# A graph layer's scatters held to TensorE's products: four waits a slot put on the GpSimd queue

## The chip, the cores and the metric

The kernel runs on one core of one Trainium2 chip. The metric is the device time of one execution in microseconds (us), and the time of a kernel is the median of its runs. PE is TensorE (PEld its weight loads), DVE is VectorE, ACT is ScalarE, POOL is GpSimd, SP is SyncE, which here only issues DMAs.

## What is computed

A message-passing layer on a graph of 6250 nodes and 100000 edges, with 128 numbers a node and 128 an edge, and a normalised residual behind it:

```python
msg_in = concatenate([x[src], x[dst], edge_attr])   # 100000 x 384
h   = msg_in @ W + b
h   = (h - mean(h)) * rsqrt(var(h) + eps) * gamma + beta
msg = relu(h)
out = segment_sum(msg, src)                         # 6250 x 128
y   = layernorm(x + out)
```

The edges come sorted by `dst`, and are summed by `src`.

## The kernel before, in words

W is three blocks, one each for `x[src]`, `x[dst]` and the edge's own numbers. The kernel first multiplies all nodes by the first two blocks (`project`). Then it takes the edges in 782 tiles of 128. Four tiles are a **slot** (`PT = 4`), so there are 196 slots, `q` = 0 to 195. The tiles also fall into five **splits** of 164, 168, 168, 164 and 118 tiles.

In each slot `edges` makes, in one PSUM bank (`hp`, two banks in turn), the part of h that needs the edge and its `dst`: first four f32 products of the loaded edge tiles `eT` with W's third block (L523, which the profile shows as eight loads and eight products), then four bf16 products of a one-hot matrix with a window of the projected nodes (L527). `scatters` has ACT copy the bank into one of eight buffers in SBUF (`hs`, L535: buffer `q % 8`), and then POOL, for each of the four tiles, copies the tile's source numbers beside its rows (L539) and issues an indirect DMA (L540), which writes the 128 rows, of 528 bytes each, to their places in a table in DRAM (`sorted`), ordered by source block. The places come from a counting sort that DVE and PE work out ahead (`places`: steps of a generator, run at slots fixed in `steps_at`; L395 and L420 are its products).

When a split's rows are all in its table, the work on pairs of source blocks begins, five slots later (`LAG = 5`). There are 25 pairs a split. Such a pair loads its rows back (`hl`, L587 on SP), and on PE it has transposes (`turn`, L617), two groups of bf16 products that add the `src` part (`pick`, L632 and L636) and the f32 products that sum the messages by source (`sums`, L677). Between them DVE and ACT compare, square, scale and add. `work(n)` emits n steps of this pipeline. A step holds a fixed part of up to four pairs at different stages, and steps are dealt out to slots by `steps_due`, about 2.4 a slot.

All engines run in the order in which the program emits their instructions. One slot of the main loop emits: loads and windows on SP, the one-hot of slot q+2 on DVE, `edges(s, q)`, the first step of pair work, `scatters(s, q)`, the steps of `places` that are due, the other one or two steps of pair work. Splits 0 to 3 are worked on in this way under later slots; the last split's pairs follow in a tail (`tail`), with the final layer norm. POOL's part in the slots is the copies and scatters alone.

Waits are found by the framework from the data: a scatter waits for ACT's copy of its slot, for POOL's copy of the numbers and for its places; ACT's copy of slot q waits for the scatters of slot q - 8, which read the same buffer; and the load of a pair waits for all scatters of its split.

Of the kernel before, what the change touches and what calls it, by code (L numbers as in the profile page):

```python
# [17 lines left out]
D = 128  # L18
# [9 lines left out]
PT = 4  # L28
WN = 42
# [54 lines left out]
def fast_path(ctx, tc, io, bad_d):  # L84
# [3 lines left out]
    nc = tc.nc  # L88
# [3 lines left out]
    psum = ctx.enter_context(tc.tile_pool(name="psum", bufs=1, space=bass.MemoryType.PSUM))  # L92

    xb_d = [dram.tile([3, hi - lo, D], BF16, name=f"xb_d{k}") for k, (lo, hi) in enumerate(TABLES)]
    drel_d = dram.tile([PIECES, PT * P], BF16, name="drel_d")
    sorted_d = [dram.tile([NB * k * P + n * P, ROW], F32, name=f"sorted{s}")
                for s, (n, k, _, _) in enumerate(SPLITS)]
# [107 lines left out]
    w = const.tile([P, 3, D], F32, name="w")  # L205
# [22 lines left out]
    sloc = const.tile([P, TILES], F32, name="sloc")  # L228
# [78 lines left out]
    xa = tabs.tile([P, NB, 3 * D], BF16, name="xa")  # L307
# [157 lines left out]
    HS, DG = 8, 2  # L465
    hs_all = [const.tile([P, PT, ROW], F32, name=f"hs{i}") for i in range(HS)]
# [4 lines left out]
    def edge_loads(q, queue=None):  # L471

        if q % DG or q >= PIECES:
            return
        t0 = q * PT
        g = min(DG, PIECES - q)
        eT = edge.tile([P, DG * PT * P], F32, name="eT", bufs=3)
        db = edge.tile([P, DG * PT * P], BF16, name="db", bufs=3)
        for n in ([(0, g)] if q else [(i, 1) for i in range(g)]):
            c0, c1 = n[0] * PT * P, min((n[0] + n[1]) * PT * P, (TILES - t0) * P)  # L480
            nc.sync.dma_start(eT[:, c0:c1], io["eT"][:, t0 * P + c0:t0 * P + c1])
            c1 = (n[0] + n[1]) * PT * P
# [28 lines left out]
        nc.vector.tensor_scalar(oh[:, :m * P], db, part_w, None, op0=ALU.is_equal)  # L511
        held["oh", q] = oh

    def edges(s, q):
        t0 = q * PT
        m = min(PT, TILES - t0)
        c0 = q % DG * PT * P
        eT = held[q // DG][0][:, c0:c0 + m * P]
        oh, win = held.pop(("oh", q)), held.pop(("win", q))
        hp = psum.tile([P, PT, P], F32, name="hp", bufs=2)  # L520
        for j in range(m):
            at = slice(j * P, (j + 1) * P)
            nc.tensor.matmul(hp[:, j, :], eT[:, at], w[:, 2, :], start=j == 0, stop=False,  # L523
                             skip_group_check=True)
        for j in range(m):
            at = slice(j * P, (j + 1) * P)
            nc.tensor.matmul(hp[:, j, :], oh[:3 * WN, at], win[:3 * WN, :],  # L527
                             start=False, stop=j == m - 1, skip_group_check=True)
        held["hp", q] = hp

    def scatters(s, q):
        t0 = q * PT
        m = min(PT, TILES - t0)
        hs, hp = hs_all[q % HS], held.pop(("hp", q))
        nc.scalar.copy(hs[:, :m, 0:D], hp[:, :m, :])  # L535
        for j in range(m):
            t = t0 + j
            parts = P if t < TILES - 1 else LAST
            nc.gpsimd.tensor_copy(hs[:, j, D:D + 1], sloc[:, t:t + 1])  # L539
            i = nc.gpsimd.indirect_dma_start(  # L540
                out=sorted_d[s][:, :],
                out_offset=bass.IndirectOffsetOnAxis(ap=place_i[:parts, t:t + 1], axis=0),
                in_=hs[:parts, j, :], in_offset=None,
            )
# [38 lines left out]
    def load_pair(s, p):  # L583

        k = 2 * SPLITS[s][1]
        pair = late["blk"].tile([P, KMAX, ROW], F32, name="hl", bufs=4)
        nc.sync.dma_start(flat(pair[:, :k, :]),  # L587
                          dram_ap(sorted_d[s], p * k * P * ROW, [[k * ROW, P], [1, k * ROW]]))
        loaded[s, p] = pair

    class Pair:
# [17 lines left out]
        def turn(self):  # L609

            self.ohn = late["blk"].tile([P, KMAX, P], BF16, name="ohn", bufs=2)
            half = self.ohe.bitcast(BF16)
            for j0, m in [(0, self.k)]:
                tr = psum.tile([P, PT, P], F32, name="tr", bufs=BANKS["tr"]).bitcast(BF16)
                tr = tr.rearrange("p t (h d) -> p (t h) d", h=2)
                for j in range(m):
                    nc.tensor.transpose(tr[:, j, :], half[:, j0 + j, 1::2], ident_h)  # L617
                self.tr = tr

        def turned(self):  # L620
# [2 lines left out]
        def pick(self, g):  # L623

            j0, m = self.groups[g]

            name = "hp" if self.s == n_split - 1 and g % 2 else "sel"
            sel = psum.tile([P, PT, P], F32, name=name, bufs=BANKS[name])
            rows = self.hl[:, j0:j0 + m, 0:D]
            on_pe = g not in BY_DVE[self.s]  # L630
            if on_pe:
                nc.tensor.matmul(sel[:, :m, :], ident, rows, start=True, stop=False)  # L632
            for j in range(m):
                b = 2 * self.p + (j0 + j) % 2
                for i in range(3):
                    nc.tensor.matmul(sel[:, j, :], self.ohn[:, j0 + j, :],  # L636
                                     xa[:, b, i * D:(i + 1) * D],
                                     start=not on_pe and i == 0,
                                     stop=(j == m - 1 and i == 2) if on_pe else i == 2)
            self.sel[g] = sel  # L640

        def rest(self, g):
# [28 lines left out]
        def sums(self):  # L671
            k = self.k
            pa_t = psum.tile([P, 512], F32, name="pa")
            self.pa = pa_t[:, :2 * ACW].rearrange("p (h d) -> p h d", h=2)
            for h in range(2):
                for j in range(h, k, 2):
                    nc.tensor.matmul(self.pa[:, h, :], self.ohe[:, j, :], self.msg[:, j, :],  # L677
                                     start=(j == h), stop=(j == k - 2 + h))

        def add(self):  # L680
            b = 2 * self.p
# [70 lines left out]
    def run(g, n=1):  # L752
        for _ in range(n):
            next(g, None)
# [3 lines left out]
    for s in range(n_split):  # L758
        t = first_tile[s]
# [466 lines left out]
```

## Time and profile before

| | |
|---|---|
| median of 3 runs | 1448.1 us (1444.97 to 1451.01) |
| the profiled execution | 1445.61 us, of which the span from the first to the last instruction is 1443.8 us |
| mean granted clock of TensorE | 0.857 of full speed |
| PE, PEld | busy 1096.7 us (76%), 902.9 us (63%) |
| POOL | busy 1007.2 us (70%), of which 775.7 us are the 782 scatters |
| DVE, ACT | busy 950.8 us (66%), 610.9 us (42%) |
| first and last scatter | start at 25.8 us and at 1277.3 us |
| tail | from about 1275 us to the end, no scatters |

How to read it: the page is one profiled execution. A group's row gives line, engine, operation, the tiles written and read, the count, the busy time and the mean of one in ns, and behind the last bar the idle time of the engine just before these instructions, with what ended most of it. "issue" as a releaser means that the engine waited for nothing that the profile shows. In a table of windows each engine has its busy time and, in brackets, how many of its instructions ran in the stretch.

### The profile page before, as it was taken

Reading aid. Unit: us, or ns where it says so; the run is one execution under the profiler, and the core shown is the slowest. Engines: PE = TensorE matmul, PEld = TensorE weight load, DVE = VectorE, ACT = ScalarE, POOL = GpSimd, SP = SyncE. Lnnn points to the kernel's source line nnn. Section 1 sums busy time; section 2 is a strip of 40 time slices with the busy share of each in tenths; the row PEclk is TensorE's granted clock in tenths of the full one; section 3 lists DMA queues with packets and bytes.
Section 4 is the critical chain, followed back from the end, with each engine's and each line's share of the span. In section 5 each row is a group of like instructions: output and inputs, shape, how many; then the busy total and the mean of one; then the engine's idle time right before and its main releaser. Section 6 shows DMA issues by size and latency. Waiting matters only on the chain.

```text
span 1443.8 us, 28271 instructions
## 1 busy us (share of the span) xinstructions
PE 1096.7 (76%) x8918; PEld 902.9 (63%) x8918; DVE 950.8 (66%) x2511; ACT 610.9 (42%) x2658; POOL 1007.2 (70%) x1681
## 2 busy tenths in 40 slices
PE   4665544468788788787888888888878988999983
PEld 3654543346566676665766666767657777777762
DVE  7885553245556676675767676766777766778995
ACT  1332211023333344443443444434445555667983
POOL 3888878887877777777777777776777766622553
PEclk9877765567877989999998998888998999999997
DMA  6899653454555644555664556656554545433431
GB/s 200 239 272 287 196 164 120 137 179 143 165 171 168 192 158 154 186 178 184 187 205 158 166 165 191 196 164 196 180 172 153 185 158 173 137 99 117 139 123 55
DMA packets 122279, 245.85 MB, mean 170 GB/s; under 512 B 46555, under 2 KB 60396, under 8 KB 122118
## 3 DMA queue, kind: packets, MB, share of 16 engines
q1 hardware_dynamic: 95956, 189.83, 43.0%
q0 software_dynamic: 25184, 53.31, 10.6%
q8 instruction: 73, 1.20, 0.3%
q10 hardware_dynamic: 978, 0.80, 0.2%
q14 instruction: 88, 0.72, 0.2%
HBM read 155.74 MB, written 88.11 MB: 169 GB/s over the span
## 4 chain that ended last, share of the span: by engine, by line
PE 53%; issue 13%; DVE 11%; POOL 10%; DMA 6%; another core or an unknown queue 2%; ACT 2%; SPq 2%; POOLq 0%; ACTq 0%; DVEq 0%
PE pa L677 16%; PE sel L636 11%; PE hp L523 10%; PE sel L632 6%; POOL sorted L540 6%; PE tr L617 4%; DMA xs<-in_xblk 3%; PE hp L527 3%; DVE sc L383 3%; PE beside L420 2%; DVE msg L668 2%; DVE ohe L605 1%; POOL hs L539 1%; DMA db<-drel_d 1%
## 5 line engine op out<-in xcount | busy, mean ns | idle before, releaser
L540 POOL DMA_INDIRECT sorted<-hs,place_i x782 | 775.7, 992 | 315.3 <-issue 221.8
L677 PE MATMUL pa<-msg,ohe 128*128 128x130 f32 x1900 | 316.0, 313 | 47.4 <-issue 29.0
L535 ACT COPY hs<-hp 128x512 f32<-128x512 f32 x196 | 113.9, 581 | 561.1 <-DMA sorted<-hs,place_i 156.9
L523 PE MATMUL hp<-w,eT 128*128 128x128 f32 x1564 | 276.9, 323 | 96.7 <-ACT hs L535 62.1
L677 PEld LDWEIGHTS pa<-msg,ohe 128*128 128x128 f32 x1900 | 272.5, 217 | 75.2 <-issue 56.4
L523 PEld LDWEIGHTS hp<-w,eT 128*128 128x128 f32 x1564 | 238.6, 228 | 115.7 <-ACT hs L535 67.5
L636 PEld LDWEIGHTS <-ohn 128*128 128x128 bf16 x2850 | 186.3, 101 | 162.8 <-issue 143.2
L653 ACT ACTIVATE sq<-sel 128x128 f32<-128x128 f32 x875 | 230.3, 282 | 108.9 <-PE sel L636 54.0
L636 PE MATMUL sel<-xa,ohn 128*128 128x128 bf16 x2625 | 214.3, 226 | 59.1 <-issue 46.9
L668 DVE SCALAR_TENSOR_TENSOR msg<-sel,rstd,cut 128x128 f32<-128x128 f32 x875 | 247.0, 344 | 8.7
L605 DVE TENSOR_TENSOR ohe<-hl,beside 128x1024 f32<-128x1024 f32 (+1 forms) x125 | 144.7, 1159 | 144.4 <-PE sel L636 47.8
L653 ACT ACTIVATION_READ_ACCUMULATOR sq<-sel 128x1 f32 x875 | 186.8, 213 | 0.0
L646 DVE TENSOR_TENSOR sel<-sel,hl 128x512 f32<-128x512 f32 x100 | 69.4, 694 | 153.2 <-remote 80.4
L539 POOL COPY hs<-sloc 128x1 f32<-128x1 f32 x782 | 165.2, 211 | 3.8
L621 ACT COPY ohn<-tr 128x1024 bf16<-128x1024 bf16 (+1 forms) x125 | 120.7, 965 | 89.9 <-PE hp L527 44.8
L632 PE MATMUL sel<-hl,ident 128*128 128x512 f32 (+1 forms) x250 | 137.1, 631 | 4.7 <-issue 3.9
L617 PE MATMUL tr<-ident_h,ohe 128*128 128x128 bf16 x950 | 93.6, 233 | 42.2 <-issue 29.6
L511 DVE TENSOR_SCALAR ohd<-db,part_w 128x512 bf16<-128x512 bf16 x194 | 70.9, 366 | 58.3 <-PE hp L527 31.3
L527 PE MATMUL hp<-win,ohd 126*128 126x128 bf16 x782 | 91.6, 240 | 13.0 <-issue 7.0
L617 PEld LDWEIGHTS <-ohe 128*128 128x128 bf16 x950 | 65.0, 104 | 56.6 <-issue 42.0
L527 PEld LDWEIGHTS <-ohd 126*128 126x128 bf16 x782 | 70.4, 110 | 25.2 <-issue 17.2
L656 ACT ACTIVATE std<-ss,eps 128x4 f32<-128x4 f32 (+1 forms) x250 | 74.3, 297 | 8.1
(157 smaller groups left out, 937.1 us busy)
## 6 DMA issues: line engine op xcount, KB each, us to landing
hl<-sorted SPq DMA_DIRECT2D x100, 528.0 KB
eT<-in_eT SPq DMA_DIRECT2D x96, 512.0 KB
sorted<-empty SPq DMA_DIRECT2D x125, 198.0 KB
db<-drel_d SPq DMA_DIRECT2D x96, 256.0 KB
sorted<-hs,place_i POOLq DMA_INDIRECT x782
hl<-sorted SPq DMA_DIRECT2D x25, 396.0 KB
win<-xb_d SPq DMA_DIRECT2D x196, 31.5 KB
xb_d<-xb SPq DMA_DIRECT2D x16, 384.0 KB
```

Of the source, the lines that this page charges most:

```text
L523: nc.tensor.matmul(hp[:, j, :], eT[:, at], w[:, 2, :], start=j == 0, stop=False, skip_group_check=True)
L527: nc.tensor.matmul(hp[:, j, :], oh[:3 * WN, at], win[:3 * WN, :], start=False, stop=j == m - 1, skip_group_check=True)
L539: nc.gpsimd.tensor_copy(hs[:, j, D:D + 1], sloc[:, t:t + 1])
L540: i = nc.gpsimd.indirect_dma_start(out=sorted_d[s][:, :], out_offset=bass.IndirectOffsetOnAxis(ap=place_i[:parts, t:t + 1], axis=0), in_=h ...
L605: nc.vector.tensor_tensor(self.ohe[:, :k, :], self.hl[:, :k, D:D + 1].to_broadcast([P, k, P]), row_bc(iota_p, k), op=ALU.is_equal)
L617: nc.tensor.transpose(tr[:, j, :], half[:, j0 + j, 1::2], ident_h)
L621: nc.scalar.copy(self.ohn[:, :self.k, :], self.tr[:, :self.k, :])
L632: nc.tensor.matmul(sel[:, :m, :], ident, rows, start=True, stop=False)
L636: nc.tensor.matmul(sel[:, j, :], self.ohn[:, j0 + j, :], xa[:, b, i * D:(i + 1) * D], start=not on_pe and i == 0, stop=(j == m - 1 and i = ...
L653: nc.scalar.activation(sq[:, j, :], self.sel[g][:, j, :], AF.Square, accum_out=ss[:, j:j + 1])
L668: nc.vector.scalar_tensor_tensor(self.msg[:, j0 + j, 0:D], self.sel[g][:, j, :], rstd[:, j:j + 1], cut, op0=ALU.mult, op1=ALU.max)
L677: nc.tensor.matmul(self.pa[:, h, :], self.ohe[:, j, :], self.msg[:, j, :], start=(j == h), stop=(j == k - 2 + h))
```

## The change

`scatters` is parted. `evict` keeps ACT's copy, and puts the slot's four tiles into a list, `waiting`. `scatter(n, tied)` takes n tiles from the head of the list and emits for each POOL's copy of its source numbers and its indirect DMA, as before. With `tied` the DMA gets one more dependency: on the last PE product that was emitted up to there (`pe` notes each product of the slots).

In slots 21 to 185 the four tiles of slot q - 1 are scattered in slot q, one at each of four points, each tied:

1. after the four f32 products of slot q (L523),
2. after its four bf16 products (L527),
3. after the first step of pair work, ahead of ACT's copy of slot q,
4. after the slot's steps of `places` and its other steps of pair work.

Slots 0 to 19 and 187 to 195 scatter their own tiles at once, untied. Slot 20 scatters nothing, and slot 186 scatters the four tiles of slot 185 and its own. The orders of PE, DVE, ACT and SP are what they were. On POOL, too, the copies and scatters come in the same order.

```diff
-    def edges(s, q):
+    def edges(s, q, half):
...
-            nc.tensor.matmul(hp[:, j, :], eT[:, at], w[:, 2, :], start=j == 0, stop=False,
-                             skip_group_check=True)
+            pe(nc.tensor.matmul(hp[:, j, :], eT[:, at], w[:, 2, :], start=j == 0, stop=False,
+                                skip_group_check=True))
+        half()
...
-    def scatters(s, q):
+    def evict(s, q):
         t0 = q * PT
         m = min(PT, TILES - t0)
         hs, hp = hs_all[q % HS], held.pop(("hp", q))
         nc.scalar.copy(hs[:, :m, 0:D], hp[:, :m, :])
-        for j in range(m):
-            t = t0 + j
+        waiting.extend((s, q, j) for j in range(m))
+
+    TIE = (20, 186)
+    waiting = []
+
+    def scatter(n, tied):
+
+        for s, q, j in waiting[:n]:
+            t = q * PT + j
             parts = P if t < TILES - 1 else LAST
-            nc.gpsimd.tensor_copy(hs[:, j, D:D + 1], sloc[:, t:t + 1])
+            nc.gpsimd.tensor_copy(hs_all[q % HS][:, j, D:D + 1], sloc[:, t:t + 1])
             i = nc.gpsimd.indirect_dma_start(
...
+            if tied:
+                tc.add_manual_dep(i.ins, last_pe[0].name, written, reason="rows behind products")
...
+        del waiting[:n]
...
             edge_hot(q + 2)
-            edges(s, q)
+            tied = TIE[0] < q < TIE[1]
+            edges(s, q, (lambda: scatter(1, True)) if tied else lambda: None)
+            if tied:
+                scatter(1, True)
             n = steps_due(q + 1) - n_steps
             work(min(n, 1))
-            scatters(s, q)
+            if tied:
+                scatter(1, True)
+            evict(s, q)
+            if not TIE[0] <= q < TIE[1]:
+                scatter(len(waiting), False)
             for g in steps_at.pop(q, []):
                 run(g)
             work(n - 1)
+            if tied:
+                scatter(len(waiting) - PT, True)
```

More of the change, by code (lines that the diff above doesn't have):

```diff
@@ L94, in fast_path, with pe @@
     xb_d = [dram.tile([3, hi - lo, D], BF16, name=f"xb_d{k}") for k, (lo, hi) in enumerate(TABLES)]
+    written = mybir.DependencyInfo(mybir.DependencyClass.Sync, mybir.DependencyReason.DATA)
+    last_pe = [None]
+    def pe(i):
+        last_pe[0] = i.ins
+        return i
     drel_d = dram.tile([PIECES, PT * P], BF16, name="drel_d")
@@ L522, in edges @@
             at = slice(j * P, (j + 1) * P)
-            nc.tensor.matmul(hp[:, j, :], eT[:, at], w[:, 2, :], start=j == 0, stop=False,
-                             skip_group_check=True)
+            pe(nc.tensor.matmul(hp[:, j, :], eT[:, at], w[:, 2, :], start=j == 0, stop=False,
+                                skip_group_check=True))
+        half()
         for j in range(m):
             at = slice(j * P, (j + 1) * P)
-            nc.tensor.matmul(hp[:, j, :], oh[:3 * WN, at], win[:3 * WN, :],
-                             start=False, stop=j == m - 1, skip_group_check=True)
+            pe(nc.tensor.matmul(hp[:, j, :], oh[:3 * WN, at], win[:3 * WN, :],
+                                start=False, stop=j == m - 1, skip_group_check=True))
         held["hp", q] = hp
-    def scatters(s, q):
+    def evict(s, q):
         t0 = q * PT
@@ L542, in scatters @@
                 out_offset=bass.IndirectOffsetOnAxis(ap=place_i[:parts, t:t + 1], axis=0),
-                in_=hs[:parts, j, :], in_offset=None,
+                in_=hs_all[q % HS][:parts, j, :], in_offset=None,
             )
+            if tied:
+                tc.add_manual_dep(i.ins, last_pe[0].name, written, reason="rows behind products")
             tc.declare_no_dep(i.ins, group=f"scatter{s}", reason="rows of different edges")
@@ L616, in turn @@
                 for j in range(m):
-                    nc.tensor.transpose(tr[:, j, :], half[:, j0 + j, 1::2], ident_h)
+                    pe(nc.tensor.transpose(tr[:, j, :], half[:, j0 + j, 1::2], ident_h))
                 self.tr = tr
@@ L635, in pick @@
                 for i in range(3):
[L636 to L639, printed above, removed]
+                    pe(nc.tensor.matmul(sel[:, j, :], self.ohn[:, j0 + j, :],
+                                        xa[:, b, i * D:(i + 1) * D],
+                                        start=not on_pe and i == 0,
+                                        stop=(j == m - 1 and i == 2) if on_pe else i == 2))
             self.sel[g] = sel
@@ L676, in sums @@
                 for j in range(h, k, 2):
-                    nc.tensor.matmul(self.pa[:, h, :], self.ohe[:, j, :], self.msg[:, j, :],
-                                     start=(j == h), stop=(j == k - 2 + h))
+                    pe(nc.tensor.matmul(self.pa[:, h, :], self.ohe[:, j, :], self.msg[:, j, :],
+                                        start=(j == h), stop=(j == k - 2 + h)))
         def add(self):
```

## The prediction

> **What bounds the kernel now.** I read the page first, for the chain and the groups.
>
> ```profile
> span 1443.8 us, 28271 instructions
> ...
> POOL 3888878887877777777777777776777766622553
> ...
> PE 53%; issue 13%; DVE 11%; POOL 10%; DMA 6%; another core or an unknown queue 2%; ACT 2%; SPq 2%; POOLq 0%; ACTq 0%; DVEq 0%
> ...
> L540 POOL DMA_INDIRECT sorted<-hs,place_i x782 | 775.7, 992 | 315.3 <-issue 221.8
> ```
>
> PE carries half of the chain, and 13% of it is "issue": PE idle with no wait to show for it. POOL is 10%, but it is busy for most of every slice until 1275 us. So I cut the span into stages by windows, and asked who waits in each.
>
> ```profile
> 100.00:410.00 310.00, 180.65 (x1145) 149.50 (x1143) 143.91 (x302) 71.33 (x222) 248.62 (x413) 0.71 0.56 174
> 410.00:1200.00 790.00, 658.25 (x5534) 537.71 (x5533) 534.63 (x1366) 350.21 (x1594) 579.14 (x969) 0.90 0.56 177
> 1200.00:1275.00 75.00, 65.57 (x596) 53.34 (x596) 47.34 (x135) 42.41 (x201) 49.89 (x86) 0.92 0.43 140
> ```
>
> ```profile
> ACT hs L535 <- DMA sorted<-hs,place_i: 144.9, 29, 8.4
> ...
> PE hp L523 <- ACT hs L535: 62.1, 20, 5.9
> ```
>
> These two waits are of 100 to 410 us. **Stage one** belongs to POOL: the scatters go back to back, ACT waits for buffers that they still read, and PE waits for ACT. The timeline, read slot by slot, has POOL seven slots behind ACT from slot 13 on (slot 30's products ran at 157.7 to 159.1 us, slot 29's scatters began at 206.2), and it has caught up at slot 64, at 408 us.
>
> **Stage two**, 410 to 1200 us, is the changed one. A scatter follows ACT's copy by a few us, and POOL pauses about every second slot. Who is late then? PE's own rows say:
>
> ```profile
> PE sel L636 <- issue: 33.5, 98, 0.5
> PE pa L677 <- issue: 25.2, 76, 1.0
> ...
> PE beside L395 <- DVE cnt L392: 11.5, 4, 4.2
> ```
>
> All "issue" rows of PE in this stage add to 98 us, all waits for other engines to 26 us. The timeline shows what such an issue wait looks like. First a group of 12 products that runs freely, then one that doesn't, then POOL beside the second:
>
> ```profile
> 691.36 0.83 PE L636 MATMUL sel<-xa,ohn 128*128 128x128 bf16 x12
> ```
>
> ```profile
> 711.97 0.33 PE L636 MATMUL sel<-xa,ohn 128*128 128x128 bf16 x3 [0.22 <-issue]
> 712.70 0.44 PE L636 MATMUL sel<-xa,ohn 128*128 128x128 bf16 x5 [0.39 <-issue]
> 713.45 0.39 PE L636 MATMUL sel<-xa,ohn 128*128 128x128 bf16 x4 [0.32 <-issue]
> 714.19 0.39 PE L636 MATMUL sel<-xa,ohn 128*128 128x128 bf16 x4 [0.35 <-issue]
> ```
>
> ```profile
> 711.00 0.98 POOL L540 DMA_INDIRECT sorted<-hs,place_i  x1 [0.28 <-POOL hs L539]
> 711.99 0.19 POOL L539 COPY hs<-sloc 128x1 f32<-128x1 f32 x1
> 712.46 0.98 POOL L540 DMA_INDIRECT sorted<-hs,place_i  x1 [0.28 <-POOL hs L539]
> ```
>
> The 12 products took 0.83 us; then about four came every 0.73 us, which is half of POOL's cycle of 0.98 + 0.19 + 0.28 = 1.45 us. To see whether it is POOL, I counted PE's weight loads in windows where the scatters do not pause:
>
> ```profile
> 615.00:639.00 24.00, 20.55 (x184) 16.40 (x183) 14.73 (x42) 8.70 (x40) 19.76 (x32) 1.00 0.49 154
> 646.00:664.00 18.00, 10.55 (x86) 7.99 (x84) 12.59 (x27) 6.20 (x30) 14.61 (x26) 0.95 0.60 201
> 926.00:948.00 22.00, 18.57 (x148) 14.52 (x145) 13.43 (x36) 8.02 (x40) 18.05 (x29) 0.92 0.49 153
> 1062.00:1085.00 23.00, 14.43 (x112) 9.80 (x109) 13.72 (x32) 5.63 (x28) 18.49 (x33) 0.93 0.43 138
> ```
>
> 521 loads in 87 us: 6.0 a us. The whole of stage two has 5533 in 790 us, 7.0 a us. POOL's idle time before its scatters there is 208.8 us for 485 of them (its group in that window); less the 0.28 us between copy and scatter each time (136 us), 73 us are true pauses, 64 of them longer than 0.1 us. So stage two is 717 us of scattering at 6.0 loads a us, 4300, and 73 us of pause, which give the other 1230: 17 a us. PE lives on POOL's pauses: a pause lets it run ahead, and the scatters starve it again. I read this as cause, not coincidence, since the stalls keep step with the scatters; the trace alone doesn't prove it.
>
> **The change, part by part.**
>
> *Order of work.* PE, DVE, ACT and SP emit what they did; evict stays where the scatters stood. Cost nothing. Each tied scatter moves past one slot of PE work. Behind it on POOL wait only later copies and scatters (POOL has no other work until the tail). Two wait for its landing. ACT's copy of slot q needs the scatters of slot q - 8, now let go in slot q - 7: six slots remain, 39 us at 6.5 us a slot, against a scatter some 8 us late. The loads of a split's rows on SP come five slots after it (first rows of split 1: issued at 564.9 us, their last scatter began at 535.7). One slot of these five goes. If that cover failed, SP's queue would stop with all edge loads behind it: in stage one SP waited 24 us so, once, and that stays.
>
> *The wait itself.* One more semaphore a scatter. The scatter's row has 806 semaphore instructions for 782 scatters, 17 ns in the median. In stage two a wait that is met costs that at most, in the shadow of the 0.28 us from copy to scatter; the 0.28 us stands in the rows with one such instruction as with a longer first one. In stage one POOL is the bound, so there it would count: slots 21 to 63, 172 scatters, 172 x 0.017 = 3 us if not hidden, 172 x 0.28 = 48 us if each tied wait cost a gap of its own. I take 0, since the gap is one of latency; 48 stays for the range. PE's signals at four more points: nothing, as L636's products that signal keep the group's pace; no row excludes a few us either way.
>
> *Stage one's ties.* Nothing else: PE is six slots past each of them, so they are met before POOL arrives.
>
> *Stage two's ties.* Slots 65 to 185 hold 484 scatters, or 484 x 1.45 = 702 us of POOL, and the change removes none. PE's loads stay 5533. By the two rates, stage two = scattering + pause, and only what PE gets out of a us of pause can alter it. The ties make three differences.
>
> First, where POOL pauses. Before, it stops for ACT's copy; now, mostly for the fourth point, the end of a slot, since the first three come within 3 us of its start and POOL needs 1.45 us for each. PE, freed by the pause, then runs to that point. That is the same trade.
>
> Second, POOL no longer works ahead while PE waits for another engine. Before, it did: tiles that were copied were scattered, and PE lost nothing. Now a PE held by DVE holds POOL too, and such a pause feeds nobody. The waits are 26 us; those of the sort's products (L395, L420: 17 us) lie ahead of the fourth point, and about half of the other 9. POOL is there waiting as often as it has caught up, 64 slots of 121. So (17 + 4.5) x 0.53 = 11 us are lost. Bounds: 0, if POOL is always behind, and 26.
>
> Third, a gain is possible: pauses may become shorter and more frequent, each at an empty queue of PE. At 17 loads a us against the free group's 12 in 0.83 us (14 a us, with what it saves up coming on top) I see no large reserve, and take 0. Its bound is in the rivals.
>
> *A rule.* The page "SBUF — State Buffer" of the Trainium skill says, under "Who interferes with whom", that PE and ACT never wait on anyone. By it the scatters couldn't slow PE, the 98 us of issue waits would be PE's own, and the sum here would be 0, with 1446 us. The rows of 711 us speak against it.
>
> *End.* From slot 186 nothing is tied. POOL then holds one slot more than before only if it was ahead; before, slot 184's last scatter ended at 1203.2 us, PE reaches slot 186 at 1203.4. The tail starts as it did: 0.
>
> Sum, against the profiled execution: 1445.6 + 11 = 1457 us. The median of the three runs lies 2.5 us over that execution, so I forecast **1458 us**.
>
> **The rivals.**
>
> *Slower by the lost pauses* (my forecast), 1458, with 1448 to 1477 as its bounds (0 to 26 us in stage two, 0 to 3 us in stage one, on 1448).
>
> *No change.* POOL's work and PE's loads are the same, and the freed PE reaches each point as soon as before it reached ACT's copy. For it: in the sum only the rate per us of pause counts. Against: the 26 us of waits. 1448.
>
> *Faster.* One mechanism: PE's issue waits. A tie gives PE a quarter slot of progress before every scatter, so it is not starved in runs of ten and more scatters. At most the 98 us could come back, but POOL needs 4 x 1.45 = 5.8 us of a slot's 6.5, so a slot can shrink by 0.7 us at most, 85 us in 121 slots. A quarter of the 98 us would be 1424. It decides once pauses come in nearly every slot and one us of them gives clearly more than 17 loads. Against it: the rate needs empty queues at the right moments, and nothing places the ties so.
>
> *Much slower.* The tied wait is not hidden and stage one grows by up to 48 us: 1496. For it: that stage has no reserve. Against: the gap of 0.28 us is the same in all rows.
>
> That the ties do nothing is true of stage one, 43 of the 165 tied slots, and is in the sum.
>
> **How the numbers follow.** About 0.5%, 7 us, is what a measurement of this kernel can tell from no change. Slower by the lost pauses 0.42, no change 0.24, faster 0.27, much slower 0.07. Part of the first case stays under 7 us, and part of the no-change case exceeds it, which about cancels: slower 0.49, within 0.24, faster 0.27. The range runs from 1422, the faster case's price, to 1482, a little over the upper bound of the first, towards the last; my own case alone would be 1448 to 1477.
>
> **What would show it.** Right: stage one's end stays near 408 us at slot 64; in 410 to 1200 us POOL's idle time before its scatters grows by about 11 us and names PE; loads per us of unbroken scatters stay near 6; ACT's copy waits for no scatter. Wrong: PE's issue waits fall well below 98 us in that stage at a shorter span (the faster case), the copy-to-scatter gap grows beyond 0.28 us in stage one, or SP's wait for a split's rows shows up behind slot 83, 125 or 166.

## The result, and the profile after

The changed kernel takes **1426.84 us** (four runs, 1423.71 to 1427.48) against 1447.28 us of the kernel before on the same chip (1444.97 to 1451.01). The ratio is **0.9852, with a 95% interval of 0.9826 to 0.9878**: faster by 20 us, where 1458 us, slower by 10, was forecast. The page of after, the lines that answer to those of before:

```profile
span 1425.2 us, 28435 instructions
...
POOL 3888878888777777777777777777777667623543
...
PE 55%; issue 14%; DVE 11%; DMA 8%; POOL 6%; SPq 4%; ACT 2%; another core or an unknown queue 1%; POOLq 0%; ACTq 0%; DVEq 0%
...
L555 POOL DMA_INDIRECT sorted<-hs,place_i x782 | 778.5, 996 | 296.4 <-issue 139.3
```

The span is 18.6 us shorter. The scatters cost what they did (778.5 us for 782), and POOL's idle time before them fell from 315.3 to 296.4 us, 18.9 us. On the chain POOL went from 10% to 6%, while "issue" did not shrink: 14% after 13%. So POOL gave something up and PE's issue waits stayed. The stages say where. Windows of after, one for each stage (columns: span, then busy time and count of PE, PEld, DVE, ACT, POOL, then the granted clock, the DMA share and GB/s):

```profile
100.00:410.00 310.00, 181.05 (x1128) 149.71 (x1126) 143.20 (x299) 71.34 (x229) 247.83 (x411) 0.69 0.57 173
410.00:1180.00 770.00, 639.81 (x5522) 523.85 (x5519) 534.27 (x1368) 349.97 (x1584) 574.74 (x965) 0.92 0.59 181
1180.00:1257.00 77.00, 67.96 (x634) 56.93 (x633) 49.41 (x142) 42.86 (x202) 54.71 (x94) 0.93 0.45 144
```

Stage one is as it was (POOL busy 247.83 us, before 248.62; PE 181.05 and 180.65). Slot by slot: slot 65 starts at 408.9 us in both kernels; slot 186 starts at 1184.1 us, before at 1203.4. All of the gain, 19.3 us, lies in the 121 slots between, and none in the tail (241.1 us from slot 186 to the end, before 240.4). These 121 slots, before and after:

```profile
408.90:1203.40 794.50, 662.00 (x5569) 540.14 (x5568) 538.22 (x1376) 353.87 (x1612) 582.79 (x975) 0.90 0.56 176
```

```profile
408.90:1184.10 775.20, 644.53 (x5572) 527.69 (x5569) 538.77 (x1377) 353.71 (x1603) 578.10 (x971) 0.92 0.58 181
```

The same 5568 loads are done in 19.3 us less. Who waits in stage two? First PE's waits of after in 410 to 1180 us, then POOL's there (line, releaser: us in total, times, longest):

```profile
PE sel L653 <- issue: 36.3, 93, 1.1
PE pa L694 <- issue: 22.0, 60, 1.1
PE tr L634 <- issue: 19.6, 50, 1.1
...
PE beside L402 <- DVE cnt L399: 8.1, 6, 2.8
```

```profile
POOL sorted L555 <- issue: 87.6, 277, 4.1
POOL sorted L555 <- POOL hs L554: 26.0, 90, 0.6
POOL sorted L555 <- PE sel L653: 22.4, 33, 1.5
POOL sorted L555 <- PE hp L535: 16.8, 24, 1.6
POOL sorted L555 <- PE tr L634: 9.7, 14, 1.3
```

All issue rows of PE add to 100 us (98 before), its waits for other engines to 23 (26 before). By its wait rows PE stalls as much as it did; what fell is its busy time in the 121 slots, 662.00 to 644.53 us for the same products. A stall shows in busy time too: the 16 products from 711.97 us on in the prediction's timeline are busy for 1.55 us, 0.10 each, the 12 of the free group for 0.07 each. What changed on POOL is who ends its pauses: now PE's products, and sooner. I read the length of each pause off the records: the time between two scatters beyond the 0.475 us of copy and gap, where it exceeds 0.1 us. In the 121 slots:

| | before | after |
|---|---|---|
| pauses | 64 | 77 |
| together, us | 81 | 63 |
| mean of one, us | 1.27 | 0.82 |
| 121 slots, us | 794.5 | 775.2 |
| 121 slots less pauses, us | 713.5 | 712.2 |

POOL's scatters with their copies are a fixed 712 us, and the 18 us of pause that are gone are the gain. That is bookkeeping: where POOL's work is fixed, any gain has to show as less pause. What made it, the experiments have to say.

### The profile page after: what moved, and what is told of

Read it like the earlier page. It is cut to its first block, busy times and chain, and to the rows that moved or that the text cites. A ratio compares the mean times of both kernels' runs of the same rounds, so it can differ in the third digit from the quotient of the medians.

```text
span 1425.2 us, 28435 instructions
## 1 busy us (share of the span) xinstructions
PE 1078.0 (76%) x8918; PEld 889.3 (62%) x8918; DVE 951.5 (67%) x2511; ACT 612.0 (43%) x2658; POOL 1006.2 (71%) x1681
## 4 chain that ended last, share of the span: by engine, by line
PE 55%; issue 14%; DVE 11%; DMA 8%; POOL 6%; SPq 4%; ACT 2%; another core or an unknown queue 1%; POOLq 0%; ACTq 0%; DVEq 0%
PE pa L694 16%; PE hp L530 11%; PE sel L653 10%; PE sel L649 6%; PE tr L634 4%; DMA xs<-in_xblk 4%; PE hp L535 3%; POOL sorted L555 3%; DVE sc L390 2%; DVE ohe L622 2%; DMA sorted<-hs,place_i 2%; PE beside L427 2%; DVE msg L685 2%; POOL y L719 1%; POOL y L759 1%
## 5 line engine op out<-in xcount | busy, mean ns | idle before, releaser
L555 POOL DMA_INDIRECT sorted<-hs,place_i x782 | 778.5, 996 | 296.4 <-issue 139.3
L530 PE MATMUL hp<-w,eT 128*128 128x128 f32 x1564 | 268.8, 315 | 101.4 <-ACT hs L543 60.7
L694 PE MATMUL pa<-msg,ohe 128*128 128x130 f32 x1900 | 307.8, 311 | 42.1 <-issue 24.6
L530 PEld LDWEIGHTS hp<-w,eT 128*128 128x128 f32 x1564 | 230.0, 220 | 121.6 <-ACT hs L543 65.1
L653 PEld LDWEIGHTS <-ohn 128*128 128x128 bf16 x2850 | 182.9, 99 | 163.6 <-issue 148.1
L653 PE MATMUL sel<-xa,ohn 128*128 128x128 bf16 x2625 | 209.0, 223 | 63.1 <-issue 55.7
L638 ACT COPY ohn<-tr 128x1024 bf16<-128x1024 bf16 (+1 forms) x125 | 120.7, 966 | 115.6 <-PE hp L535 53.4
L554 POOL COPY hs<-sloc 128x1 f32<-128x1 f32 x782 | 161.2, 206 | 3.8
L634 PE MATMUL tr<-ident_h,ohe 128*128 128x128 bf16 x950 | 90.3, 231 | 43.1 <-issue 27.3
L535 PEld LDWEIGHTS <-ohd 126*128 126x128 bf16 x782 | 69.1, 108 | 24.4 <-issue 18.9
```

Source lines behind the costliest of these rows:

```text
L530: pe(nc.tensor.matmul(hp[:, j, :], eT[:, at], w[:, 2, :], start=j == 0, stop=False, skip_group_check=True))
L535: pe(nc.tensor.matmul(hp[:, j, :], oh[:3 * WN, at], win[:3 * WN, :], start=False, stop=j == m - 1, skip_group_check=True))
L554: nc.gpsimd.tensor_copy(hs_all[q % HS][:, j, D:D + 1], sloc[:, t:t + 1])
L555: i = nc.gpsimd.indirect_dma_start(out=sorted_d[s][:, :], out_offset=bass.IndirectOffsetOnAxis(ap=place_i[:parts, t:t + 1], axis=0), in_=h ...
L634: pe(nc.tensor.transpose(tr[:, j, :], half[:, j0 + j, 1::2], ident_h))
L638: nc.scalar.copy(self.ohn[:, :self.k, :], self.tr[:, :self.k, :])
```

## The experiments

**What they are to tell apart.** Theory A: the waits end POOL's pauses sooner, after a quarter slot of PE's work and not after ACT's copy, and a shorter pause serves PE as well. Theory B: the waits do nothing; the gain comes from emitting the scatters a slot later, at four places. Theory C: the gain belongs to one of the four points alone. Behind them stands a question that the prediction left open: do the scatters cause PE's issue waits?

The chips differ: the kernel before took 1477.2 us on the one of the first four experiments (the second chip, below) and 1346.5 to 1347.5 us on those of all others, so every ratio is against the kernel before on the same chip. A profile of the kernel before was taken on the first chip alone.

### Which wait does it

`x1_untied` emits everything at the four points but adds no wait:

```diff
-            if tied:
+            if False:
                 tc.add_manual_dep(i.ins, last_pe[0].name, written, reason="rows behind products")
```

> The changed kernel with the scatters emitted at the four points, but without the added waits. Theory A (the gain is in POOL's pauses, which now end at a product of PE and no longer at ACT's copy): no wait, no gain, the time of the kernel before, 1447 us within 5, and POOL's idle time before its scatters back near 209 us in stage two. Rival B (emitting the scatters a slot later is the change, not the wait): 1427 us. Rival C (TensorE's granted clock happened to be better): the clock decides, near 0.87 and 1427 us.

`x2_first` ties only the scatter at point 1 (`scatter(1, False)` at points 2 and 3, `False` at the fourth):

> Only the first of the four points is tied (the four f32 products of the next slot); the other three scatters follow freely. One hold a slot in place of four. Theory A, if any hold that ends at a PE product will do: near 1427 us, with pauses once a slot. If the pause must also be cut into parts: half the gain, about 1437. Rival C: no order in the times, clock and time move together.

`x3_last` ties only what is let go at point 4:

> Only the fourth point is tied, the end of a slot's pair work. By the working of the prediction POOL stands there most often, so this one wait should carry nearly all of the effect: 1427 to 1432 us. If several short holds are what counts: about 1437 us.

`x4_three` ties points 1 to 3, not the fourth:

```diff
-                scatter(len(waiting) - PT, True)
+                scatter(len(waiting) - PT, False)
```

> Points one to three are tied, the fourth is free. If the fourth point carries the effect: 1440 us and more. If holds at any point do: 1427 to 1432 us.

Measured, ratios to 1477.2 us:

| | us | ratio, 95% interval | slots 65 to 164, us | pauses there: number, us | PE's issue waits there, us |
|---|---|---|---|---|---|
| x1_untied | 1476.57 | 0.9987 [0.9956, 1.0017] | 665.4 | 53, 84.7 | 115 |
| x2_first | 1454.23 | 0.9846 [0.9791, 0.9900] | 653.1 | 59, 66.7 | 101 |
| x3_last | 1455.39 | 0.9871 [0.9811, 0.9931] | 646.4 | 61, 61.9 | 98 |
| x4_three | 1447.96 | 0.9809 [0.9753, 0.9864] | 644.9 | 60, 59.9 | 100 |
| before, first chip | 1447.28 | 1 | 646.9 | 49, 61.9 | 84 |
| after, first chip | 1426.84 | 0.9852 [0.9826, 0.9878] | 633.4 | 60, 45.5 | 89 |

Theory B falls with x1: the later emission alone gives nothing that shows. Theory C falls with x2 and x3: either end of the slot, alone, gives as much as the whole change did on the first chip, and three points give about as much. It takes a wait on PE once a slot; which product it is matters little. Whether more holds give a little more is not settled: x4 lies 6 us under x2, its four runs at 1446.17 to 1451.76 us and those of x2 at 1451.74 to 1455.76. POOL's group of scatters in slots 65 to 164 (its idle time stands behind the second bar), x1 and then x3:

```profile
L555 POOL DMA_INDIRECT sorted<-hs,place_i x397 | 393.3, 991 | 193.6 <-issue 148.2 <-POOL hs L554 39.9 <-ACT hs L543 2.2
```

```profile
L555 POOL DMA_INDIRECT sorted<-hs,place_i x399 | 394.1, 988 | 166.4 <-issue 103.7 <-POOL hs L554 32.4 <-ACT hs L543 13.9
```

27.2 us less idle time before as many scatters; the slots are 19.0 us shorter (the pauses by my count 22.8). In every row of the table the slots' time less the pauses is 581 to 588 us: that is 400 scatters at 1.455 us, 582 us, which the change can't touch. These slots take that sum and what POOL pauses.

On PE's side this chip shows what the first didn't: its issue waits fall with the ties. In slots 65 to 185 they are 132 us in x1 and 116, 111 and 114 in x2 to x4, that is 16 to 21 of the 20 to 29 us by which these slots are shorter (818.6 us in x1, then 798.6, 790.1 and 790.1).

The granted clock went up beside the gain on the first chip (0.90 to 0.92 in the slots). It doesn't make the gain, as runs at a like mean clock over the span show: on the first chip one run of the changed kernel had 0.855 and took 1426.71 us, where the kernel before took 1445.61 at 0.857; on the second chip runs at 0.843 took 1483.33 us before, 1453.42 in x2 and 1448.21 in x4.

**Why a shorter pause is enough.** For each pause in slots 65 to 185 I counted the loads that it gave: all loads from its start to the start of the next pause, less 6.0 for each us between them in which POOL scattered. By chip, since the two stall unequally (first chip: before and after; second: x1 to x4; 137 of 141 and 298 of 306 pauses, as the last ones of each profile are left out):

| pause, us | first chip: pauses, mean us | loads it gave | a us | second chip: pauses, mean us | loads it gave | a us |
|---|---|---|---|---|---|---|
| 0.1 to 0.5 | 28, 0.21 | -1.3 | | 44, 0.22 | 1.8 | |
| 0.5 to 0.8 | 34, 0.71 | 18.6 | 26 | 16, 0.69 | 12.8 | 19 |
| 0.8 to 1.1 | 21, 0.96 | 22.4 | 23 | 76, 0.98 | 19.5 | 20 |
| 1.1 to 1.4 | 12, 1.27 | 27.9 | 22 | 85, 1.22 | 18.5 | 15 |
| 1.4 to 1.7 | 29, 1.58 | 24.7 | 16 | 36, 1.58 | 21.6 | 14 |
| 1.7 to 2.2 | 11, 1.82 | 26.3 | 14 | 24, 1.89 | 19.0 | 10 |
| over 2.2 | 2, 3.59 | 38.5 | 11 | 17, 2.84 | 26.7 | 9 |

Single pauses scatter widely (standard deviations of 9 to 15 loads). The trend is the same on both chips all the same: up to about 1 us the yield grows, and from there to 2 us it hardly does, 22 to 28 loads on the first chip and 19 to 22 on the second. On the first chip the short pauses are mostly those of after and the long ones those of before, so length isn't parted there from the place at which a pause falls. Before, a pause ended with ACT's copy (47 of the 64 ended 0.7 to 0.8 us after the copy's end), which stands behind a group of products and ACT's squares of it; of its 64 pauses 34 were of 1.5 us and more, and what lay beyond 1 us bought little. After, four are so long. One pause of each kind, in the timelines of POOL, before and then after (start, duration, instruction, in brackets the idle time ahead):

```profile
737.71 0.98 POOL L540 DMA_INDIRECT sorted<-hs,place_i  x1 [2.05 <-issue]
```

```profile
1139.72 0.98 POOL L555 DMA_INDIRECT sorted<-hs,place_i  x1 [1.23 <-remote]
1140.71 0.19 POOL L554 COPY hs<-sloc 128x1 f32<-128x1 f32 x1
1141.17 0.98 POOL L555 DMA_INDIRECT sorted<-hs,place_i  x1 [0.28 <-PE hp L530]
...
1146.23 0.98 POOL L555 DMA_INDIRECT sorted<-hs,place_i  x1 [0.97 <-remote]
```

The 2.05 us of the first are 1.77 us beyond the usual gap of 0.28; those after are 0.95 and 0.69 beyond it, 6.5 us apart. The same can be read by time. From the start of a pause to 7 us behind its end PE issued 8.1 loads a us, before and after; later than that, 5.2. More pauses and shorter ones leave less of the late time: 289 us of the 121 slots before, 236 after. The table of yields fits a stock of instructions that fills in a pause and is used up under the scatters; no record shows such a stock, so that is an inference.

### Do the scatters cause the stalls?

`x5_none` takes the kernel before and issues no scatters in slots 65 to 165:

```diff
+            if 64 < q < 166:
+                continue
             i = nc.gpsimd.indirect_dma_start(
...
-                          dram_ap(sorted_d[s], p * k * P * ROW, [[k * ROW, P], [1, k * ROW]]))
+                          dram_ap(sorted_d[0 if s < 4 else s], p * k * P * ROW, [[k * ROW, P], [1, k * ROW]]))
```

> The kernel before without the scatters of slots 65 to 165 (POOL only copies the source numbers there; pairs of splits 1 to 3 read back split 0's rows, so that all that is read has been written). If the scatters starve PE: PE's issue waits of 98 us in stage two fall below 20 us in the slots without scatters, and those 101 slots take about 5.6 us each in place of 6.6, so the span falls by 80 to 120 us. If PE's issue waits are its own: they stay, and the span falls by less than 20 us.

`x6_memset` puts two memsets on POOL in the place of each such scatter (`nc.gpsimd.memset(filler, 0.0)` and one of 300 columns, ahead of the `continue`):

> As the kernel without the scatters of slots 65 to 165, but POOL fills a scratch tile in the place of each scatter, two memsets of 1.27 us in all, so that it is as busy as with scatters and has no pauses. If it is POOL's being busy that starves PE: issue waits as before or more, slots of 6.6 us or longer. If it is the scatter's own work, writing and running DMA descriptors: the span is that of the kernel without scatters, within 10 us.

`x7_even` keeps the scatters and adds a memset of one column ahead of each, in slots 65 to 185:

> The kernel before with one more small memset on POOL ahead of each scatter of slots 65 to 185, 0.1 us each, 48 us in all, so that part of the pauses is spread evenly over the scatters, without any wait for PE. If evenly spread short gaps between scatters feed PE as well as the ties do: 1425 to 1440 us. If only full pauses refill PE, or a memset starves it like a scatter: POOL's 48 us come on top, up to 1490 us.

x5 took 1169.25 us (one run), 4.62 us a slot (slots 65 to 164) and no issue wait. But this chip answered before the experiment could: x7 is the kernel before with a short memset, and its profile has no issue waits either. It took 1347.55 us against 1346.9, ratio 1.0012 [0.9999, 1.0026]. The memset was to add time to each scatter's cycle, and added none, since it ran in the gap between copy and scatter. The timeline of POOL in x7:

```profile
600.08 0.19 POOL L540 COPY hs<-sloc 128x1 f32<-128x1 f32 x1
600.20 0.10 POOL L542 MEMSET filler<- 128x1 f32 x1
600.54 0.98 POOL L543 DMA_INDIRECT sorted<-hs,place_i  x1 [0.25 <-POOL filler L542]
```

So x7 tests nothing. x6 (1352.8 us, one run) kept POOL as busy with other work, at 4.99 us a slot without an issue wait; then, at slot 166, the real scatters came behind memsets that were still to run, and PE stood still (the window, then ACT's waits in the whole of x6, one of them 115.3 us long):

```profile
960.00:1080.00 120.00, 37.42 (x374) 32.99 (x374) 32.71 (x103) 28.76 (x137) 107.09 (x210) 0.65 0.18 57
```

```profile
ACT hs L536 <- DMA sorted<-hs,place_i: 358.7, 60, 115.3
```

Its total says nothing, and its slots nothing about issue waits on a chip that has none. To try again, I ran the changed kernel itself beside a repeat of x5, an earlier release without waits, and fewer copies.

`y3_after` is the changed kernel, unaltered:

> The changed kernel, unaltered, on whichever chip this call gets, as the measure for the other three. Theory A (pauses of POOL that end sooner feed PE as well as long ones): 0.98 to 0.99 of the kernel before, if PE shows issue waits here, and POOL's pauses shorter than before; where PE shows none, 1.00. Rival C (the clock): no tie between the time and the pauses.

`y4_none` repeats x5:

> The kernel before without the scatters of slots 65 to 165 once more (pairs of splits 1 to 3 read back split 0's rows), beside kernels with scatters on the same chip. If the scatters starve PE: where the others show issue waits of PE of 80 us and more in these slots, this one shows under 10 us. If the waits are the chip's own: they stay.

y4 took 1171.55 us. y3 took 1348.99 us, ratio **1.0001 [0.9990, 1.0012]**: on this chip the change is worth nothing. Its profile tells why. Windows and POOL's group of y3 in slots 65 to 164, then PE's three longest waits there:

```profile
372.80:970.10 597.30, 462.59 (x4384) 406.67 (x4381) 434.82 (x1088) 273.59 (x1240) 479.74 (x800) 0.92 0.62 194
```

```profile
L555 POOL DMA_INDIRECT sorted<-hs,place_i x400 | 399.5, 999 | 115.9 <-POOL hs L554 81.8 <-PE hp L530 7.7 <-PE pa L694 5.8
```

```profile
PE sel L653 <- ACT ohn L638: 53.5, 23, 5.9
PE sel L649 <- DVE msg L685: 42.3, 18, 5.1
PE beside L402 <- DVE cnt L399: 16.5, 6, 6.7
```

There is no issue row among all its waits there (134 us). POOL's idle time is 115.9 us for 400 scatters, 0.29 each: nearly all of it the gap of 0.28 us. POOL pauses 11 times, 8.3 us together, and 597.3 us is again the 582 of 400 scatters and a little more. Here POOL, back to back, is the bound; the ties are met before it comes, as in stage one of the first chip. And PE runs a group freely in the midst of scatters, first PE and then POOL of y3:

```profile
608.10 0.83 PE L653 MATMUL sel<-xa,ohn 128*128 128x128 bf16 x12
```

```profile
608.08 0.98 POOL L555 DMA_INDIRECT sorted<-hs,place_i  x1 [0.28 <-POOL hs L554]
```

Twelve products took 0.83 us with a scatter running beside all of them; on the first chip, beside scatters, four came every 0.73 us. Counted from 7 us after a pause to the next one, PE issued 5.2 loads a us on the first chip (before and after alike), on the second 4.0 in x1 and 4.2 to 4.9 in x2 to x4, and 7.7 in y3. The granted clock doesn't part the first chip from this one: x7 has a mean of 0.857, as the kernel before on the first chip.

For the same question the kernel without scatters ran on two more chips.

> The kernel before without the scatters of slots 65 to 165, as y4_none. On a chip where the kernel before takes 1440 us and more, and its PE shows 80 us and more of issue waits in these slots: under 10 us of issue waits if the scatters starve PE, 80 us if the waits belong to the chip alone.

> The kernel before without the scatters of slots 65 to 165, a last time, for a chip whose PE shows issue waits with them (the kernel before takes 1440 us and more there; on the others it took 1347). Under 10 us of issue waits in these slots if the scatters starve PE, about 80 us if the waits are the chip's own. On a chip of the other sort: 1168 us again, and nothing learnt.

1167.48 and 1168.15 us, where the kernel before took 1347.01 and 1346.52: both chips were of the kind without issue waits. All that these four runs without scatters (x5, y4, z1, w1) show is what the scatters cost there, 176 to 180 us in 101 slots. On a chip that stalls, the kernel without scatters never ran.

The profiles of the stalling chips do hold a stretch without scatters: the tail, where PE works on the last split's pairs with the same groups of products. All waits of PE in the kernel before on the first chip, from the end of its last scatter (1278.2 us) on:

```profile
PE pa L677 <- DVE acc L685: 5.7, 4, 3.2
PE pa L677 <- DVE msg L668: 5.4, 12, 0.7
PE sel L636 <- ACT ohn L621: 0.4, 2, 0.2
```

There is no issue wait in 1241 products; the 5568 products of slots 65 to 185 had 287. x1 to x4 have none in their tails either, and after has one of 0.3 us. The last 1000 products of the kernel take 118.3 to 121.5 us on both sorts of chip (119.2 in before, 120.7 in y3). So the waits don't belong to the chip alone: they come with the work of the slots and end with it. They also keep step with the scatters: of those 287, six end between 0.3 and 0.6 us after a scatter's start, though 960 of the 5568 products start there. This speaks for the scatters as the cause, but other work ends with them (the DMA engines are busy for 0.56 of the slots and 0.34 of the tail), so it isn't shown.

### A release earlier in the slot, and fewer copies

`y1_early` takes the kernel before and, in slots 65 to 185, emits ACT's copy and the scatters ahead of the first step of pair work, with no wait: the other way to end POOL's pauses sooner.

```diff
+            if 64 < q < 186:
+                scatters(s, q)
             work(min(n, 1))
-            scatters(s, q)
+            if not 64 < q < 186:
+                scatters(s, q)
```

> The kernel before, with ACT's copy and the scatters of slots 65 to 185 emitted ahead of the slot's first step of pair work instead of behind it. No tie to PE. Theory A: POOL's pause ends at ACT's copy, which no longer stands behind a step's squares on ACT, so pauses get shorter, and the time falls like that of the ties, to 0.98 to 0.99 of the kernel before. If the tie to PE itself is what helps (a scatter that starts just behind products): no gain, 1.00.

> The kernel before with ACT's copy ahead of the slot's first step, as y1_early. Where PE shows issue waits: by theory A POOL's pauses get shorter without any tie and the time falls to 0.98 to 0.99 of the kernel before; if the tie itself is what helps, 1.00. Where it shows none: 1.00, as y1_early.

> ACT's copy ahead of the slot's first step, without a tie. Where PE shows issue waits: 0.98 to 0.99 of the kernel before if a sooner end of the pause is what counts, 1.00 if it is the tie. Elsewhere 1.00.

Three chips: 1347.3 us at 0.9994 [0.9980, 1.0008], 1347.91 at 1.0006 [0.9997, 1.0016], 1346.31 at 1.0001 [0.9991, 1.0012]. No difference, and none is to be had where POOL has hardly a pause. The kernel never met a chip that stalls, so whether a sooner pause without a wait on PE would do is not settled.

`y2_onecopy` goes at what bounds these chips, POOL's cycle. The four copies of source numbers become one of four columns, ahead of the first scatter; ahead of the others stands a memset of one column on a tile that nobody reads, in slots 65 to 185:

```diff
+    filler = const.tile([P, 1], F32, name="filler")
...
-            nc.gpsimd.tensor_copy(hs[:, j, D:D + 1], sloc[:, t:t + 1])
+            if not 64 < q < 186:
+                nc.gpsimd.tensor_copy(hs[:, j, D:D + 1], sloc[:, t:t + 1])
+            elif j == 0:
+                nc.gpsimd.tensor_copy(hs[:, :m, D:D + 1], sloc[:, t:t + m].unsqueeze(2))
+            else:
+                nc.gpsimd.memset(filler, 0.0)
```

> The kernel before, where POOL copies the source numbers of a slot's four tiles at once ahead of its first scatter, in slots 65 to 185, with a memset of one column between two scatters in place of the copy. The 0.28 us from a copy to its scatter falls away three times a slot. If PE is starved per scatter (the DMA's descriptors): POOL's pauses grow by what the gaps gave up, PE gets the same in sum, and the time is 0.98 to 1.00. If the gaps between scatters fed PE: slower, 1.01 to 1.03.

> One copy of the source numbers a slot in slots 65 to 185, as y2_onecopy, which was 0.943 where PE showed no issue waits and POOL set the pace. Where PE is starved per scatter: POOL's freed time turns into pauses, 0.97 to 1.00. If the gaps fed PE: 1.01 and more.

1273.42 us at **0.9434 [0.9417, 0.9451]**, and 1272.75 at 0.9459 [0.9434, 0.9484] on the next chip. The timeline of POOL in y2, and the windows of slots 65 to 164:

```profile
600.68 0.11 POOL L545 MEMSET filler<- 128x1 f32 x1
600.99 0.97 POOL L546 DMA_INDIRECT sorted<-hs,place_i  x1 [0.19 <-issue]
```

```profile
373.80:918.50 544.70, 446.04 (x4383) 394.31 (x4381) 431.41 (x1088) 273.40 (x1241) 457.40 (x803) 0.94 0.67 212
```

A scatter that follows an instruction it doesn't depend on starts 0.19 us after it, not 0.28, and 0.11 us of memset replace 0.19 of copy: a cycle of 1.28 us for 1.455. This holds for three of a slot's four scatters; the one behind the copy keeps 1.45. Three are 0.53 us, and 121 slots give 64 us. 74 came: from slot 65's first scatter to slot 186's it is 723.0 us in y3 and 648.6 in y2. Most of the other 10 us lies in cycles longer than the usual, of which y2 has fewer; no run shows why.

`z4_onecopy_tied` is the changed kernel with one copy in each slot, from slot 0 on; `w3_onecopy_tied` is the same on another chip:

```diff
+    filler = const.tile([P, 1], F32, name="filler")
...
-            nc.gpsimd.tensor_copy(hs_all[q % HS][:, j, D:D + 1], sloc[:, t:t + 1])
+            m = min(PT, TILES - q * PT)
+            if j == 0:
+                nc.gpsimd.tensor_copy(hs_all[q % HS][:, :m, D:D + 1], sloc[:, t:t + m].unsqueeze(2))
+            else:
+                nc.gpsimd.memset(filler, 0.0)
```

> The changed kernel with its ties and one copy a slot, in all slots. If both effects add: on a chip without issue waits 0.91 to 0.94 of the kernel before (stage one is POOL's too), on a chip with them 0.93 to 0.97, by stage one's 300 us at 5.0 in place of 5.8 us a slot and the ties' 1.5%.

> The ties with one copy a slot, in all slots, which was 0.913 where PE shows no issue waits. Where it shows them: 0.93 to 0.97 if PE is starved per scatter, 0.98 and more if in proportion to the time in which the gaps between scatters are missing.

1230.24 us at **0.9134 [0.9112, 0.9156]**, and 1230.84 at 0.9144 [0.9128, 0.9161]. It beats both kernels, on chips without issue waits; on one with them it wasn't measured. The windows of slots 65 to 164 in z4:

```profile
340.80:882.20 541.40, 446.17 (x4385) 394.19 (x4382) 430.50 (x1085) 273.15 (x1241) 450.93 (x801) 0.94 0.67 213
```

Against y2, slot 65 starts 33.0 us sooner, since stage one, which POOL bounds on every chip, now has the short cycle too. The slots themselves are 3.3 us shorter (541.4 and 544.7): the ties add little here, one profile against one.

## Why the prediction was wrong

*The step that failed* is the third difference of the ties: that pauses could become "shorter and more frequent, each at an empty queue of PE" was named, and taken as 0, because 17 loads a us of pause seemed to leave no reserve. That took the yield of a pause as proportional to its length. By the table above it isn't. By the prediction's own sum, with slots 65 to 185 and 6.0 loads a us of scattering: before, 5568 loads less 6.0 x 713.5 are 1287 from 81 us, 16 a us; after, 5569 less 6.0 x 712.2 are 1296 from 63 us, 21 a us. The same loads out of 18 us less. The term that stood at 0 was worth -19 us. (The loads of the prediction's four windows add to 524, not 521; the rate stays 6.0.) The trace of before held a hint, which I passed over by using the mean alone: by the count of the table, its 20 pauses of 0.5 to 1.5 us (1.04 in the mean) gave 22 loads each, its 33 longer ones (1.67) gave 25, so 60% more pause for 13% more loads.

*The second difference*, 11 us lost because a PE held by DVE also holds POOL, did not come. POOL's idle time before its scatters, which was to grow by 11 us, fell: 208.8 us for 485 scatters in 410 to 1200 us before, and after, in 410 to 1180 us,

```profile
L555 POOL DMA_INDIRECT sorted<-hs,place_i x483 | 479.5, 993 | 193.2 <-issue 87.6 <-POOL hs L554 26.0 <-PE sel L653 22.4
```

A loss inside the gain can't be excluded; it has no row of its own. That the pauses would name PE was right.

*The first difference* called the new end of a pause "the same trade". It is the trade that paid, and the fourth point, though POOL pauses there most often (40 of 77), isn't what makes it: x4, without it, gains as much.

*The faster rival* had the right number, 1424 us, and its mechanism, that PE's issue waits come back, is half borne out. On the first chip they stayed (98 us before, 100 after), and the time came out of PE's busy rows; on the second chip most of the gain is issue waits (132 us in x1, 111 to 116 in x2 to x4). Its deciding condition was half met: one us of pause gave more than 17 loads, but pauses came in 77 cases for 121 slots, not in nearly every slot.

*Right* were the steps costed at nothing in stage one (slot 64's scatters within 2 us of where they were), the wait itself (the gap stays 0.28 us), SP's queue (one wait of 24.1 us for a split's rows in both kernels), the end, and the starved rate as unchanged: 5.2 loads a us from 7 us after a pause on, before and after alike on the first chip (on the second it was 4.0 in x1 and 4.2 to 4.9 with ties). ACT's copy did wait more for scatters than the prediction allowed, 34.2 us in ten waits where it had been 12.0 in two, and nobody behind it was late: PE has no row for that copy in stage two.

*The rule on PE*, from the Trainium skill's page "SBUF — State Buffer", section "Who interferes with whom", says of the ports of SBUF that PE and ACT never wait on anyone. By it alone the forecast would have been no change. The chips of all runs from x5 on look as it says, with no issue wait beside 400 scatters in y3. On the first chip and that of x1 to x4 PE has 84 to 115 us of issue waits in 100 slots. What holds PE there, a memory port or the supply of its instructions, no run here shows.

**Shown**: the waits make the gain (x1 against x2 to x4, on one chip), any hold a slot gives it (x2, x3, x4), the clock doesn't (runs at like clocks), it is gone on a chip where POOL has hardly a pause and PE no issue waits (y3), and the issue waits end with the slots' work. **Argued**: that a shorter pause serves PE as well since what it refills saturates. **Open**: whether the scatters cause the issue waits, why one chip has them and another doesn't, and whether `y1_early` or one copy would gain on a chip that stalls.

## What to carry to other kernels

Where one engine lives on another's pauses, sort the pauses by length and ask what each gives before taking a mean rate: if the yield levels off, ending pauses sooner is a gain though nothing is removed. A wait added to an engine that has caught up can be free and can even pay, but only where that engine has pauses; where it runs back to back, shorten its cycle instead. A gain that rests on a stall should be measured on more than one chip, since chips can differ in it. And before building a kernel without the suspect, look for a stretch of the profile that already lacks it: the tail said more here than four runs without scatters.

## What the runs showed of the hardware

- One kernel, the one before, took 1346.5 to 1347.5, 1447.3 and 1477.2 us on different chips, its runs on each within 0.6% of their median there. The granted clock doesn't explain it: 0.857 for the first and for x7 (the slowest had 0.832 to 0.851). The slower ones show issue waits of PE in step with POOL's scatters, and none worth naming once the scatters have ended; there the last 1000 products take 118 to 122 us on all.
- On POOL, a scatter starts 0.28 us after a copy that it depends on and 0.19 us after a memset that it doesn't; a memset of one column (0.10 us) between copy and scatter lengthened nothing.
- One copy of four columns and three memsets in the place of four copies, in 121 of the 196 slots, was worth 5.4 to 5.7% where POOL was the bound, more than the change studied here.
